# Heads: projections step first in a round, and those of tiles 2 to 4 begin two tiles ahead, with their queries in a score buffer

## The chip, the cores and the metric

The kernel runs on one core of a Trainium2 chip. A core has five engines that take their instructions in order from queues of their own and meet at semaphores: TensorE (matmuls, transposes), VectorE, ScalarE, GpSimd, and SyncE, which here only issues DMA transfers. The metric is device time in microseconds for one launch, the median of the runs. All data are fp32.

## The reference

Two layers act on 3327 nodes of 256 features: a graph convolution, a mixture of experts, a graph attention, and last a block of attention heads, which is all that the change touches:

```python
# x: (3327, 256), layer-normed; 4 heads (n), 4 experts (e) of queries per head, d = 64
sx = einsum('bsh,ndh->bnsd', x, hl_w) + hl_b
q  = einsum('bnsd,neod->bneso', sx, wq)
k  = einsum('bnsd,nod->bnso', sx, wk)
v  = einsum('bnsd,nod->bnso', sx, wv)
scores = einsum('bnesd,bntd->bnest', q, k) * d**0.5 + causal
att = softmax(scores, axis=-1)
qkv = einsum('bnest,bntd->bnesd', att, v)          # zero where sx is zero
# then a gate over the 4 experts, residual, layer norm, a two-layer FFN with
# residual and layer norm, and a softmax gate over the heads
```

The mask is causal: a tile of rows sees only itself and the tiles before it. So the work grows along the sequence, and the first tiles have very little.

## The kernel before

The rows are padded to 3328 and cut into 26 tiles of 128. The earlier layers leave their result in a DRAM tensor `xs`; then `heads` (line 854) runs the block. It writes every instruction in the order in which it is to stand: the wrapper `InOrder` chains each engine's instructions, so that each engine's queue is the order of the program, and line 61 (inside the wrapper) is the line of all of them in the profile. Tiles have to be told apart by names.

**Projections.** `prepare(t, res)` (line 907) makes what tile t needs. It is a generator with nine steps between its `yield`s: 1, load the rows (`xres`, a SyncE transfer); 2, their mean and variance on VectorE (`pst`, `pmv`, `prs`); 3, the norm on GpSimd (`prs`, `xn`); 4, transpose on TensorE, and copy (`pt`, `xt`); 5, the heads' input (`psxt`, `sxt`), and its nonzero mask `nz` by two ScalarE operations; 6, four transfers that lay the mask out as `sxd`, and the values (`pv`, copied to `v`); 7, the keys (`pk`, copied to `kt`), and four transfers of `v` to the DRAM tensor `vs`; 8, the queries (`pq`, copied with a factor 8 to `qt`); 9, the transpose of `sxt` back to rows (`sx`), and `res.update(...)`, which makes "qt" a key of the tile's entry in `ready`. `empty` (line 877) gives each copy to ScalarE or VectorE by a running sum of their loads. Some buffers are single: `xn` and `nz` share one tag with one buffer, so `xn` of a next tile can be written only when the transfers that read the last `nz` are over. `xt` and `v` are single, `sxt` and `xres` double, `sxd` triple, `qt` double.

**Attention.** A unit is a head of a tile (lines 1374, 1375), in order of tiles. Its keys are cut in `t // 4 + 1` chunks of up to 512 columns. For a chunk, `fill` makes the scores of the four experts on TensorE (`pqk`, four PSUM banks), `drain` brings them to a score buffer `sc` on VectorE with their maximum (a masked form for the last chunk), `weigh` takes the exponential on ScalarE, `turn` transposes 32x32 blocks on VectorE in place, `values` loads the values from `vs` to `vr`, and `attend` multiplies on TensorE into `po`. After a unit's last chunk `over` masks `po` into `ot`, and `back` transposes it (`ptO`) and copies it (`qkv`, `glp`). The pool `scp` has nine score buffers, of 4x512 numbers a partition. One pool `psm` of four PSUM banks serves `pqk` and all other small matmuls.

**Tails.** When a tile's four heads are through, `tail` (line 1193), again a generator, makes gate, norms, FFN and output, mostly on GpSimd and ScalarE.

**Order.** The main loop (line 1422) is one round per chunk: drain ahead as far as `wanted` says (three chunks, and `t // 4` more), attend, turn the next chunk, load and weigh the second next, `back` of the unit that has ended, one step of the tails and one of the projections, the rest of the weighing, and one `fill` if none is left. For tiles below 8 tails and projections step in every round, later only in rounds that follow no unit's end. `begin(u)` (line 1376) is called by the first `fill` of a unit. For the first head of a tile it steps the tile's generator until it is over, and starts that of the next tile. A tile of the first four has four rounds, so half of the nine steps of `prepare` are left to this forced end; tiles 4 to 7 have eight rounds.

Of the kernel before, what the change touches and what calls it, by code (L numbers as in the profile page):

```python
# [12 lines left out]
F32 = mybir.dt.float32  # L13
# [9 lines left out]
P = 128  # L23
N = 3327
NT = 26
# [3 lines left out]
BLK = 512  # L29
# [72 lines left out]
class Net:  # L102
# [751 lines left out]
    def heads(self, xs, vs, out):  # L854
# [3 lines left out]
        with ExitStack() as ctx:  # L858
            one = ctx.enter_context(tc.tile_pool(name="at", bufs=1))
            self.work = ctx.enter_context(tc.tile_pool(name="atw", bufs=2))  # L860
            scp = ctx.enter_context(tc.tile_pool(name="ats", bufs=9))
            vrp = ctx.enter_context(tc.tile_pool(name="atv", bufs=3))
            tl = ctx.enter_context(tc.tile_pool(name="att", bufs=2))
# [43 lines left out]
            def prepare(t, res):  # L907
# [63 lines left out]
                        in_=v[ds(Q * b, Q), :, :],  # L971
                    )
                yield
                qt = tl.tile([P, 4, 2, P], F32, tag="qt", name="qt")
                pp = [ps.tile([P, 2, 2, P], F32, tag="b", name="pq") for _ in range(2)]
                for c in range(2):
                    for i in range(2):
# [13 lines left out]
            def run(gens):  # L991

                gens[:] = [g for g in gens if next(g, None) is None and g.gi_frame is not None]

            tails, preps, ready = [], [], {}

# [48 lines left out]
            def weigh(u, g, experts):  # L1047

                n = span(u["t"], g)[1] * P
                q = ready[u["t"]]  # L1050
                if u["h"] == g == 0 and 0 in experts:
                    q["den"] = sm.tile([P, 16, 7], F32, tag="den", name="aden", bufs=2)
                for k in experts:
                    e = u["sc"][g][:, k, :n]
                    nc.scalar.activation(
                        e, e, AF.Exp, bias=u["nmax"][:, k : k + 1],
                        accum_out=q["den"][:, 4 * u["h"] + k, g : g + 1],
                    )
                    load["act"] += 0.26 + 0.00088 * n

            def values(u, g):

                lo, n = (4 * i for i in span(u["t"], g))
                v = u["v", g] = vrp.tile([P, 16, 64], F32, tag="vr", name="vr")
                for q in range(4):
                    nc.sync.dma_start(out=v[ds(Q * q, Q), :n, :], in_=vs[u["h"], :, lo : lo + n, :])

            def turn(u, g):


                n = span(u["t"], g)[1] * P
                w = u["sc"][g][:, :, :n]
                nc.vector.transpose(w, w)
                load["dve"] += 0.1 + 0.00417 * n
# [7 lines left out]
            def attend(u, g):  # L1082


                t = u["t"]
                w, v = u["sc"][g], u["v", g]
                lo, n = (4 * i for i in span(t, g))
                for b2 in range(0, n, 2):
                    for k in range(2):
                        for q in range(4):  # L1090
                            r, b = ds(Q * q, Q), b2 + k

                            after = 4 * t + q - lo
                            if b > after and t:
                                continue
                            nc.tensor.matmul(
                                po[ds(64 * k, 64), q, :, :], v[r, b, :], w[r, :, ts(b, Q)],
                                start=(g == b2 == 0), stop=(b + 2 > after if t else b2 == 2),
                            )

            def over(u):

                u["ot"] = tl.tile([P, 4, P], F32, tag="ot", name="ot", bufs=1)
                to = u["ot"].rearrange("p e (q i) -> p q e i", q=4)
                there = u["sxd"][:, u["h"] : u["h"] + 1, :]
                if u["t"] < 5 or u is units[-1]:

                    nc.vector.tensor_tensor(
                        to, po,
                        there.rearrange("p o (q i) -> p q o i", q=4).to_broadcast([P, 4, 4, Q]),  # L1110
                        ALU.mult,
                    )
                    load["dve"] += 0.7
                else:
                    nc.scalar.copy(to, po)
                    nc.gpsimd.tensor_tensor(
                        u["ot"], u["ot"], there.to_broadcast([P, 4, P]), ALU.mult
                    )
                    load["act"] += 0.6

            def back(u):


                h = u["h"]
                r = ready[u["t"]]
                if h == 0:
                    r["qkv"] = tl.tile([P, 4, 4, 64], F32, tag="qkv", name="qkv", bufs=2)
                    r["glp"] = sm.tile([P, 4, 4, 4], F32, tag="glp", name="glp", bufs=3)
                pt = ps.tile([P, 4, 68], F32, tag="b", name="ptO")
                for e in range(4):  # L1130
                    nc.tensor.matmul(
                        pt[:, e, :], u["ot"][:, e, :], igw[:, h, e, :], start=True, stop=True
                    )
                nc.scalar.copy(r["qkv"][:, h, :, :], pt[:, :, :64])
                nc.scalar.copy(r["glp"][:, h, :, :], pt[:, :, 64:])
                load["act"] += 0.55
                if u["t"] == NT - 1:
                    if h % 2:
                        tails.append(last_tail(u["t"], h // 2, u["sx"], r))
                elif h == 3:  # L1140
                    while len(tails) > 4:
                        run(tails)
                    tails.append(tail(u["t"], u["sx"], r["qkv"], r["glp"], r["den"]))
# [232 lines left out]
            def begin(u):  # L1376

                t = u["t"]
                if u["h"] == 0:
                    while preps:  # L1380
                        run(preps)
                    if t == 0:
                        for _ in prepare(0, ready.setdefault(0, {})):
                            pass
                    if t + 1 < NT:
                        preps.append(prepare(t + 1, ready.setdefault(t + 1, {})))
                u.update(ready[t])

            filled = drained = 0
# [1 line left out]
            def fill_next():  # L1391
                nonlocal filled
                if filled < len(chunks):
                    u, g = chunks[filled]
                    if g == 0:
                        begin(u)
                    fill(u, g)
                    filled += 1

            def drain_to(n):  # L1400
                nonlocal drained
                while drained < min(n, len(chunks)):
                    if filled == drained:
                        fill_next()
                    drain(*chunks[drained])
                    drained += 1

            def wanted(k):

                return k + 3 + chunks[min(k + 2, len(chunks) - 1)][0]["t"] // 4  # L1410
# [11 lines left out]
            for k, (u, g) in enumerate(chunks):  # L1422
                ahead = chunks[k + 2] if k + 2 < len(chunks) else None
                drain_to(wanted(k))
                attend(u, g)
                if k + 1 < len(chunks):
                    turn(*chunks[k + 1])
                if ahead:
                    values(*ahead)
                    if ahead[1]:  # L1430
                        weigh(*ahead, range(2))
                if ended:
                    back(ended)
                last = u if g == u["t"] // 4 else None
                if last:
                    over(u)
                if not ended or u["t"] < 8:
                    run(tails)
                    run(preps)
                ended = last  # L1440
                if ahead:
                    weigh(*ahead, range(2 if ahead[1] else 0, 4))
                if filled == drained:
                    fill_next()
# [556 lines left out]
```

## Time and profile before

| what | value |
| --- | --- |
| median of 3 runs | 2971.8 us (2970.73 to 2976.79) |
| the profiled execution's own time | 2971.83 us |
| its span | 2970.1 us |
| TensorE busy | 2662.9 us, 90% |
| VectorE busy | 2398.0 us, 81% |
| ScalarE busy | 1813.9 us, 61% |
| GpSimd busy | 973.8 us, 33% |
| mean granted TensorE clock | 0.973 |
| first instruction of the heads | 973.41 us, the transfer of `xres` |

In the profile PE is TensorE's matmuls, PEld its loads of weights, DVE is VectorE, ACT ScalarE, POOL GpSimd, and SPq the transfers that SyncE issues. A line of the view in order of time has the start and the length in us, engine, line, operation, what is written and what is read with shapes, and how many; in brackets stands how long the engine was idle before it, and what it was released by. A group merges instructions that follow each other. A matmul of fp32 data appears twice in the counts[...]. Ends of matmuls are modelled, so TensorE's busy time is not time at its peak rate.

The main loop follows no clock: which engine waits is decided by the order of queues, and by buffers.

### The profile page before, as it was taken

The numbers are of one execution on the slowest core, as the hardware profiler recorded it, in microseconds if no ns is written. First come the engines' busy times: TensorE is split into PE (matmuls) and PEld (weight loads), VectorE is DVE, ScalarE is ACT, GpSimd is POOL, SyncE is SP. The second block draws the span as 40 slices with busy tenths as digits, with TensorE's granted clock in tenths as the row PEclk, the third lists the DMA queues.
The fourth block names the chain that finished last, engine by engine and source line by source line (L and its number), as shares of the span: only waits on it lengthen the run. The fifth ranks groups of instructions, "written<-read, shape, count | busy, mean of one in ns | idle before, by whom it ended". The sixth has DMA issues, their size and how long they took to land. (4 is left out here: it accounts for less than half of the span.)

```text
span 2970.1 us, 125328 instructions
## 1 busy us (share of the span) xinstructions
PE 2662.9 (90%) x53422; PEld 1966.3 (66%) x53422; DVE 2398.0 (81%) x5619; ACT 1813.9 (61%) x5128; POOL 973.8 (33%) x1448
## 2 busy tenths in 40 slices
PE   7999988879889788899999999999989999999996
PEld 6878887657668666566666666666666666656664
DVE  5102643689999577789999999999999999999997
ACT  6410135555555457677777776777777677676674
POOL 6441635622231146544433332322222222122121
PEclk9999999999999789999999999999999999999997
DMA  9994568648775222333333443443433433343432
GB/s 377 355 321 135 185 220 276 226 159 285 243 251 169 56 77 77 104 100 106 114 107 104 116 115 106 115 114 112 122 112 113 117 114 114 111 118 110 117 109 77
DMA packets 258188, 449.70 MB, mean 151 GB/s; under 512 B 58816, under 2 KB 156608, under 8 KB 257504
## 3 DMA queue, kind: packets, MB, share of 16 engines
q1 hardware_dynamic: 245536, 417.50, 45.6%
q0 software_dynamic: 6576, 18.02, 1.7%
q8 instruction: 421, 6.90, 1.0%
q10 hardware_dynamic: 5520, 6.18, 0.7%
q14 instruction: 135, 1.11, 0.1%
HBM read 393.37 MB, written 25.88 MB: 141 GB/s over the span
## 5 line engine op out<-in xcount | busy, mean ns | idle before, releaser
L61 ACT ACTIVATE sc<-sc,anmax 128x512 f32<-128x512 f32 (+3 forms) x1568 | 1040.4, 668 | 109.6 <-DVE anmax L61 109.4
L61 PEld LDWEIGHTS po<-sc,vr 32*64 32x64 f32 x43728 | 662.8, 131 | 395.2 <-DVE sc L61 234.0
L61 PE MATMUL po<-sc,vr 32*64 32x128 f32 x43728 | 765.2, 275 | 117.7 <-DVE sc L61 72.3
L61 DVE STREAM_TRANSPOSE sc<-sc 128x2048 f32<-128x2048 f32 (+3 forms) x392 | 816.2, 2082 | 24.2 <-ACT sc L61 23.9
L61 PE MATMUL pqk<-kt,qt 64*128 64x512 f32 (+3 forms) x3136 | 776.2, 579 | 24.5 <-ACT qt L61 4.8
L61 DVE TENSOR_SCALAR_CACHE_REDUCE sc<-pqk 128x512 f32<-128x512 f32 (+2 forms) x1152 | 655.5, 623 | 76.7 <-PE pqk L61 74.7
L61 PEld LDWEIGHTS pqk<-kt,qt 64*128 64x128 f32 x3136 | 319.2, 187 | 247.0 <-issue 102.5
L61 PE MATMUL acc<-wh,p 128*128 128x259 f32 x1352 | 310.0, 387 | 34.5 <-DVE p L61 34.4
L61 PEld LDWEIGHTS acc<-wh,p 128*128 128x128 f32 x1352 | 254.1, 190 | 92.7 <-DVE p L61 52.2
L61 PE MATMUL acc<-y,pan 128*128 128x256 f32 x1352 | 303.5, 385 | 12.2 <-DMA pan<-in_adjt_dram 10.5
L61 POOL TENSOR_TENSOR ot<-ot,sxd 128x512 f32<-128x512 f32 x83 | 105.7, 1273 | 601.1 <-ACT ot L61 588.2
L61 ACT ACTIVATION_READ_ACCUMULATOR sc<-sc,anmax 128x1 f32 x1568 | 299.4, 191 | 0.0
L61 PEld LDWEIGHTS acc<-y,pan 128*128 128x128 f32 x1352 | 257.8, 192 | 53.0 <-issue 17.5
L61 DVE CUSTOM_DVE_ANT_0 sc<-pqk,mask 128x512 f32<-128x512 f32 (+3 forms) x416 | 242.1, 636 | 38.4 <-PE pqk L61 38.0
L61 ACT ACTIVATE u<-u,d 128x512 f32<-128x512 f32 (+1 forms) x182 | 125.2, 688 | 159.4 <-DVE u L61 159.3
L61 DVE SCALAR_TENSOR_TENSOR u<-bc,d 128x512 f32<-128x512 f32 (+1 forms) x182 | 136.4, 750 | 0.1
L61 DVE SCALAR_TENSOR_TENSOR p<-pan,u 128x512 f32<-128x512 f32 (+1 forms) x182 | 126.9, 697 | 10.2 <-PE acc L61 6.1
L61 ACT COPY qkv<-ptO 128x256 f32<-128x256 f32 x104 | 38.5, 370 | 153.3 <-PE ptO L61 153.0
L61 ACT ACTIVATE junk<-ar 128x1664 bf16<-128x1664 f32 x52 | 82.7, 1591 | 65.9 <-DMA ar<-in_adj_dram 64.8
L61 PE MATMUL ptO<-igw,ot 128*128 128x68 f32 x832 | 117.2, 284 | 5.5 <-issue 2.3
L61 PEld LDWEIGHTS ptO<-igw,ot 128*128 128x128 f32 x832 | 102.4, 193 | 24.1 <-issue 17.5
L61 DVE CUSTOM_DVE_ANT_0 sg<-sg,dst 128x1664 bf16<-128x1664 bf16 (+2 forms) x56 | 99.9, 1791 | 1.2 <-ACT dst L61 1.0
(336 smaller groups left out, 2976.6 us busy)
## 6 DMA issues: line engine op xcount, KB each, us to landing
vr<-vs SPq DMA_DIRECT2D x976, 128.0 KB
ar<-in_adj_dram SPq DMA_DIRECT2D x104, 832.0 KB
vr<-vs SPq DMA_DIRECT2D x544, 96.0 KB
pan<-in_adjt_dram SPq DMA_DIRECT2D x156, 256.0 KB
pan<-in_adjt_dram SPq DMA_DIRECT2D x26, 1024.0 KB
pan<-in_adjt_dram SPq DMA_DIRECT2D x20, 832.0 KB
w1e<-w SPq DMA_DIRECT2D x59, 256.0 KB
took<-places SPq DMA_DIRECT2D x59, 129.0 KB
```

What stands on the lines that cost most here:

```text
L61: made = make(*args, **kw)
```

## The change

`run(preps)` now stands ahead of `run(tails)` in a round. Tiles 2, 3 and 4 have their generators started two tiles ahead (that of tile 2 together with that of tile 1, four rounds later); from tile 5 on it is one tile ahead as before. `begin` steps all running generators only until the tile that begins has its queries, no longer until all are over. The queries of tiles 0 to 4 are put into a buffer of the score pool, half of which they use, so that three tiles' queries can be alive at once.

```diff
@@ prepare
-                qt = tl.tile([P, 4, 2, P], F32, tag="qt", name="qt")
+                if t < AHEAD:
+                    qt = scp.tile([P, 4, BLK], F32, tag="sc", name="qts")[:, :, : 2 * P]
+                    qt = qt.rearrange("p h (i q) -> p h i q", i=2)
+                else:
+                    qt = tl.tile([P, 4, 2, P], F32, tag="qt", name="qt")
@@ heads
             tails, preps, ready = [], [], {}
+            AHEAD = 5
+            def later(n, gen):
+                for _ in range(n):
+                    yield
+                yield from gen
@@ begin
                 if u["h"] == 0:
-                    while preps:
-                        run(preps)
                     if t == 0:
                         for _ in prepare(0, ready.setdefault(0, {})):
                             pass
-                    if t + 1 < NT:
-                        preps.append(prepare(t + 1, ready.setdefault(t + 1, {})))
+                    while preps and "qt" not in ready[t]:
+                        run(preps)
+                    begun = [t + 1] if AHEAD <= t + 1 < NT else []
+                    if t + 2 < AHEAD:
+                        begun = [t + 2] if t else [1, 2]
+                    for i, n in enumerate(begun):
+                        preps.append(later(4 * i, prepare(n, ready.setdefault(n, {}))))
@@ the main loop
                 if not ended or u["t"] < 8:
+                    run(preps)
                     run(tails)
-                    run(preps)
```

The profile of the changed kernel calls the queries of tiles 0 to 4 `qts`.

## The prediction

> **What bounds the kernel now.** I read the page's slices first, then stretches cut at the tiles of the last stage, then TensorE and VectorE in order of time across one tile boundary, and last the waits on `xn`. The chain of waits on the page reaches back only over the last tenth of the span, so it says nothing on the place of the change.
>
> The slices (74.3 us each; tenths of VectorE busy, then TensorE's granted clock):
>
> ```profile
> DVE  5102643689999577789999999999999999999997
> PEclk9999999999999789999999999999999999999997
> ```
>
> From slice 18 (1337 us) to the last but one VectorE is at nine tenths or more; there is hardly anything to win there. The stage of the heads begins at 973 us, and its first five slices stand at 5, 7, 7, 7, 8, with the clock at 7 and 8 in two of them. Cut from one tile's first score matmul to the next one's (columns: stretch, length, then busy time and count of PE, PEld, DVE, ACT, POOL, then clock, DMA share, GB/s):
>
> ```profile
> 1010.45:1032.99 22.54, 19.71 (x272) 15.73 (x272) 14.80 (x55) 13.49 (x52) 1.74 (x3) 0.83 0.26 69
> 1032.99:1061.30 28.31, 22.88 (x376) 17.56 (x376) 19.44 (x57) 17.10 (x61) 10.91 (x16) 0.84 0.28 77
> 1061.30:1095.30 34.00, 27.59 (x511) 20.04 (x511) 23.71 (x57) 20.91 (x67) 11.66 (x17) 0.85 0.28 79
> ```
>
> These are tiles 1, 2, 3. VectorE idles 7.74, 8.87 and 10.29 us, TensorE 2.83, 5.43 and 6.41. The idle time is nearly one piece per tile, the forced end of `prepare`; here from tile 2 to tile 3:
>
> ```profile
> 1053.24 0.65 DVE L61 TENSOR_TENSOR ot<-po,sxd 128x512 f32<-128x512 f32 x1
> 1053.88 2.07 PE L61 MATMUL psxt<-xt,hlt 128*128 128x128 f32 x8 [2.49 <-ACT xt L61]
> 1056.54 1.22 PE L61 MATMUL pv<-wv,sxt 128*128 128x128 f32 x4 [0.58 <-ACT sxt L61]
> 1057.69 1.23 PE L61 MATMUL pk<-sxt,wk 64*128 64x128 f32 x8
> 1058.70 1.92 PE L61 MATMUL pq<-sxt,wq 64*128 64x128 f32 x16
> 1060.65 1.08 ACT L61 ACTIVATE qt<-pq 128x512 f32<-128x512 f32 x2 [1.06 <-PE pq L61]
> 1061.30 2.57 PE L61 MATMUL pqk<-kt,qt 64*128 64x512 f32 x8
> 1063.05 0.69 DVE L61 CUSTOM_DVE_ANT_0 sc<-pqk,mask 128x512 f32<-128x512 f32 x1 [9.15 <-PE pqk L61]
> ```
>
> VectorE stops for 9.15 us while TensorE walks a serial chain. The same gap opens tiles 1, 2 and 4, with 8.09 (plus 1.28 and 1.06), 7.03 and 9.28 us.
>
> Later a second, smaller wait: TensorE stands at the transpose of `xn`, which GpSimd makes late (tiles 6 to 9: 1.92, 4.80, 3.85, 1.41 us). The seventh and eighth:
>
> ```profile
> 1206.20 0.69 PE L61 MATMUL pt<-ident,xn 128*128 128x128 f32 x2 [4.80 <-POOL xn L61]
> 1208.50 0.56 DVE L61 TENSOR_SCALAR_CACHE_REDUCE sc<-pqk 128x384 f32<-128x384 f32 x1 [3.01 <-PE pqk L61]
> 1257.51 0.69 PE L61 MATMUL pt<-ident,xn 128*128 128x128 f32 x2 [3.85 <-POOL xn L61]
> 1260.24 0.69 DVE L61 TENSOR_SCALAR_CACHE_REDUCE sc<-pqk 128x512 f32<-128x512 f32 x1 [3.44 <-PE pqk L61]
> ```
>
> [...] `psxt` takes 2.07 us in the gaps and 1.06 in the running stream (1265.55), the pair of transposes 0.69 against 0.44. [...] the first `xres`, issued at 973.41, released VectorE at 975.45, 2.04 us.
>
> **The change, part by part.** No instruction is added but a few queue entries; order and one buffer differ.
>
> (1) *Tile 1, a loss.* The forced rounds at `begin(1)` now also step tile 2's generator. In TensorE's queue the transpose of `xn` of tile 2 and its `psxt` come to stand ahead of tile 1's first scores. That `xn` has the single buffer which `nz` of tile 1 holds until its four `sxd` transfers have landed. They were issued 1006.86 to 1009.41; plus 2.0 is 11.4, plus two GpSimd operations of 0.60 and 0.61 gives 1012.65. TensorE, done with `pq` at 1009.77, waits 2.9 us; then transposes 0.69, `xt` copy 0.37 and hand-over 0.1, `psxt` 2.07: scores at 1015.85 instead of 1010.45. **+5.4.** Queued behind it are tile 1's scores, so VectorE as well. If the nz buffer came free early this is +3; with a late landing +8.
>
> (2) *Tile 1 to 2.* Before, first drain to first drain was 1011.60 to 1033.94 = 22.34, of it 7.03 gap and 15.3 VectorE work in an unbroken row. Now the rest of tile 2's projections and the first steps of tile 3's lie in these rounds: TensorE +0.7 (`pv`), +0.7 (`pk`), +1.2 (`pq`), +0.9 (two pairs of transposes), at running-clock durations. A round is `pqk` 1.3, `po` 1.2, `ptO` 1.1 = 3.6 on TensorE against 3.4 to 5 on VectorE; the additions lengthen it by about 1.2 in all. 16.5 against 22.3: **−5.8**, which just pays for (1).
>
> (3) *Tile 2 to 3.* 29.11 before, 9.15 gap, 20.0 work without a break. TensorE's 22.88 busy contains the chain at half clock, 6.5 to 7.1 us by its rows (2.07+1.22+1.23+1.92+0.69), which become 4.1 in the stream (1.06+0.69+0.72+1.16+0.44). Rounds stretch by 0.6 (round 1: 3.7+1.06 against 4.1). One forced round stays at `begin(3)`: `sx` of tile 3 and `psxt` of tile 4, the latter waiting for an `xt` copied behind two `qts` copies (1.08+0.37). VectorE's cover is transpose and `ot`, 2.4; 2 us remain open. 22.6: **−6.5**.
>
> (4) *Tile 3 to 4.* 33.50 before, 9.28 gap; 24.2 work, rounds of 6 us against TensorE's 4.7 to 5.1 plus 0.4 to 1.2: hidden. +0.5 for stretching: **−8.8**. At tile 5 the forced `pq` remains; ScalarE's `kt` copies (0.63) leave the wait behind `nzf`: **−0.5**, of a gap of 7.10.
>
> (5) *Projections first, tiles 6 to 9.* In the built order `prs` and `xn` stand ahead of seven operations of the second norm (GpSimd 1199.88 to 1204.32, 4.4 us; for tile 6 ten, 6.7). The waits 1.92, 4.80, 3.85, 1.41 fall to 0, 0.4, 0, 0: 11.6 us of TensorE. VectorE's gaps right after are 0.55, 3.01, 3.44, 1.03 = **−8.0** (bounds −5 and −11.6). What is late next is the norm, by 1.8 us; two empty rounds stand before its transpose, so nobody waits.
>
> (6) *Score buffers, SyncE.* At most three of nine buffers hold queries; four chunks of scores are alive in tiles 0 to 3, five in tile 4. Nobody waits: 0. Without that room VectorE would wait a round, 4 us. On SyncE the `vr` loads pass behind four `sxd` (2.6) or four `vs` issues (2.0), but are wanted two rounds later, 7 us: 0; without that cover 2 us per tile, three times.
>
> (7) *From tile 5 on* the order within a round changes on ScalarE and GpSimd alone: 0, with −5 and +6 as ends (rivals).
>
> Sum: 5.4 −5.8 −6.5 −8.8 −0.5 −8.0 = **−24.2**. The profiled execution took 2971.83 (span 2970.1), the same as the median 2971.8; so 2947.6, say **2948**.
>
> **Rivals.**
>
> *TensorE becomes the bound of tiles 1 to 3.* For: it is busy 19.71 of 22.54. If its busy time does not shrink, its idle 2.83+5.43+6.41 = 14.7 is all there is, less 5.4, and half of (5): −13, **2959**. Against: some 7 us of each tile were chain at half clock. A weaker form, in which the 5.4 grows to 10, leaves −8.
>
> *It doesn't do what it says.* Forced rounds remain, and the gap only moves to where `xt`, `kt` or a bank is awaited, as tile 5's 7.10 shows with all its rounds. Then (3), (4) and (5) shrink to a third, 7.8, against +5.4 −5.8: −8 or less, **2966** to 2972.
>
> *Slower: ScalarE waits in order.* A projection's copy now stands ahead of a tail's work that is ready, so ScalarE waits for the matmuls of that step: 4.5 us a tile (1.06+0.7+0.7+1.16+0.44+0.44), 21 tiles, 94.5 at most. From 26% of it reaching VectorE (24.2) the gain is gone; a third, 31.5, gives **2979**. For: ScalarE's `qkv` copies wait for TensorE's `ptO` already, 77.5 us past 1400 us. Against: it is busy 61%, and past 1330 us VectorE waited for ScalarE's `sc` for only 14.7 us, so there is slack.
>
> *More than forecast:* (1) at +3 and (5) at its full 11.6, with tile 3's round hidden: −32, **2940**.
>
> **How the numbers follow.** The forecast (2938 to 2960, the first rival's number inside) 0.67; above 35 us of gain 0.06; the weak gain, 2960 to 2966, 0.14; within 0.2% (6 us, about what a measurement of this kernel can tell from no change) 0.07; slower 0.06. Faster: 0.67+0.06+0.14 = 0.87. The range for 8 in 10 is 2935 to 2963: it leaves out half of the weak gains, the unchanged, the slower, and a tail of the large gains.
>
> **What would show it.** VectorE's gaps at the first drains of tiles 2, 3 and 4 below 3 us; that of tile 1 grown from 8 towards 16, with TensorE waiting there for GpSimd's `xn`; `psxt` at about 1.06 us from tile 3 on; waits of `pt` on `xn` in tiles 6 to 9 near zero; tile 4's first drain some 16 us earlier, tile 10's some 24, and the shift constant after. Wrong if tile 1's gap passes 25 us, if new VectorE gaps on ScalarE's `sc` appear past 1330 us, or if a drain waits for a score buffer.

## The result

The changed kernel takes 2943.3 us (median of five runs, 2939.7 to 2954.3) against 2971.8 of the kernel before (2963.2 to 2976.8). The ratio is 0.9916, with an interval from 0.9889 to 0.9943. In a second set of runs it was 2946.6 against 2974.5, ratio 0.9907 [0.9890, 0.9923]. Faster, then: the medians differ by 28 us, where 24 were forecast.

To see where they come from I use one mark for each tile: the start of VectorE's first masked drain of that tile, counted from the start of the first `xres` transfer, with which the stage of the heads begins. The stages ahead of it hold the same code in all kernels here, yet in fourteen profiled executions the heads began anywhere from 972.9 to 981.6 us. Marks counted from the stage's own start leave that out. The change against before, in us:

| mark | before | change | difference | change, second execution |
|---|---|---|---|---|
| tile 1 | 38.19 | 42.78 | +4.6 | +4.4 |
| tile 2 | 60.53 | 59.08 | −1.5 | −1.9 |
| tile 3 | 89.64 | 83.31 | −6.3 | −6.7 |
| tile 4 | 124.58 | 109.81 | −14.8 | −15.2 |
| tile 5 | 170.86 | 156.65 | −14.2 | −14.0 |
| tile 10 | 433.52 | 408.69 | −24.8 | −25.4 |
| tile 13 | 632.67 | 608.37 | −24.3 | −24.1 |
| tile 16 | 877.55 | 844.60 | −33.0 | −30.8 |
| end | 1996.72 | 1964.06 | −32.7 | −32.8 |

The profiled execution of the change spans 2941.6 us, 28.5 less than before: 32.7 won in the heads, 4.2 lost in the stages ahead, which the change doesn't touch.

The slices of the page of the kernel after, VectorE's busy tenths and TensorE's granted clock:

```profile
DVE  5102643589999587889989999999999999999997
PEclk9999999999999799999999999999999999999998
```

The first slices of the heads (the fourteenth on) stood at 5, 7, 7, 7, 8 and stand at 5, 8, 7, 8, 8; the clock is held down in one slice instead of two. Cut into stretches close to the first score matmuls of the tiles (columns as before: stretch, length, busy time and count of PE, PEld, DVE, ACT, POOL, then clock, DMA share, GB/s), tiles 1, 2, 3 of the kernel after:

```profile
1019.10:1035.50 16.40, 16.15 (x267) 12.69 (x265) 14.06 (x53) 10.93 (x40) 1.74 (x3) 0.98 0.35 93
1035.50:1060.00 24.50, 21.62 (x389) 16.66 (x389) 20.60 (x59) 16.91 (x62) 6.82 (x9) 1.00 0.39 108
1060.00:1087.00 27.00, 25.14 (x511) 17.95 (x511) 24.40 (x60) 20.50 (x67) 9.94 (x14) 1.00 0.33 90
```

They took 22.54, 28.31 and 34.00 us. (The cuts are rounded, and the last one lies 2.8 us behind tile 4's first scores, at 1084.24, so the third stretch is a little too long here.) VectorE's busy time is about what it was (14.80, 19.44, 23.71); its idle time fell from 7.74, 8.87, 10.29 to 2.34, 3.90, 2.60. The granted clock rose from 0.83 to 0.85 there to 0.98 and 1.00. In the chains of projections at the old gaps of tiles 2, 3 and 4 (1026.05 to 1032.20, 1053.90 to 1060.70 and 1087.45 to 1094.50 in the kernel before) it had been 0.53, 0.50 and 0.50.

The same in order of time, the lines that answer to those shown of before. First the start of tile 1, which is now later, then the first drains of tiles 2 and 3 and the gap that stays at tile 5:

```profile
1015.02 0.61 POOL L61 TENSOR_TENSOR xn<-xres,pmv 128x256 f32<-128x256 f32 x1 [8.66 <-DMA sxd<-nz]
1016.38 0.69 PE L61 MATMUL pt<-ident,xn 128*128 128x128 f32 x2 [3.00 <-POOL xn L61]
1017.52 2.08 PE L61 MATMUL psxt<-xt,hlt 128*128 128x128 f32 x8
1019.53 1.48 PE L61 MATMUL pqk<-kt,qts 64*128 64x256 f32 x8
1020.36 0.42 DVE L61 CUSTOM_DVE_ANT_0 sc<-pqk,mask 128x256 f32<-128x256 f32 x1 [2.41 <-PE pqk L61]
...
1036.65 0.56 DVE L61 CUSTOM_DVE_ANT_0 sc<-pqk,mask 128x384 f32<-128x384 f32 x1 [0.29 <-PE pqk L61]
...
1058.63 1.16 PE L61 MATMUL psxt<-xt,hlt 128*128 128x128 f32 x8 [0.85 <-ACT xt L61]
1060.88 0.69 DVE L61 CUSTOM_DVE_ANT_0 sc<-pqk,mask 128x512 f32<-128x512 f32 x1 [2.05 <-PE pqk L61]
...
1128.74 0.56 DVE L61 TENSOR_SCALAR_CACHE_REDUCE sc<-pqk 128x384 f32<-128x384 f32 x1 [6.79 <-PE pqk L61]
```

`xn` of tile 2 waits for the four `sxd` transfers out of `nz`, TensorE waits 3.00 us for `xn`, and tile 1's scores stand behind it. The gaps of 7.03 and 9.15 us at tiles 2 and 3 are 0.29 and 2.05; at tile 4 there is none; tile 5's 7.10 is 6.79.

### The profile page after: what moved, and what is told of

Same layout as the page of the kernel before. It is cut to its first block, busy times and chain, and to the rows that moved or that the text cites. A ratio compares the mean times of both kernels' runs of the same rounds, so it can differ in the third digit from the quotient of the medians.

```text
span 2941.6 us, 125324 instructions
## 1 busy us (share of the span) xinstructions
PE 2652.3 (90%) x53422; PEld 1963.2 (67%) x53422; DVE 2398.5 (82%) x5619; ACT 1811.3 (62%) x5128; POOL 973.1 (33%) x1448
## 3 DMA queue, kind: packets, MB, share of 16 engines
q14 instruction: 135, 1.11, 0.1%
## 5 line engine op out<-in xcount | busy, mean ns | idle before, releaser
L61 PE MATMUL pqk<-kt,qt 64*128 64x512 f32 (+1 forms) x2944 | 738.4, 582 | 18.6 <-ACT qt L61 5.3
L61 PEld LDWEIGHTS pqk<-kt,qt 64*128 64x128 f32 x2944 | 299.3, 185 | 230.3 <-issue 99.2
L61 DVE CUSTOM_DVE_ANT_0 sc<-pqk,mask 128x512 f32<-128x512 f32 (+3 forms) x416 | 242.3, 636 | 24.2 <-PE pqk L61 23.7
```

The source lines that it names most:

```text
L61: made = make(*args, **kw)
```

## Experiments

Each ran beside the kernel before; the medians are of 4 to 16 executions. The edits are told below. The three kernels with masks of tails apart (the one with tiles 6 and 7 ahead is one of them) also have `nz` of tile 1 apart and tile 5 ahead.

| kernel | median us | ratio to before, interval |
|---|---|---|
| the change | 2943.34 | 0.9916 [0.9889, 0.9943] |
| exchange only | 2958.20 | 0.9944 [0.9929, 0.9959] |
| early start only | 2965.31 | 0.9974 [0.9966, 0.9983] |
| `nz` of tiles 0 to 4 apart | 2946.32 | 0.9908 [0.9892, 0.9925] |
| tile 5 ahead too | 2947.11 | 0.9909 [0.9895, 0.9923] |
| projections first from tile 10 on | 2960.71 | 0.9950 [0.9937, 0.9962] |
| `nz` of tile 1 apart | 2943.96 | 0.9893 [0.9878, 0.9907] |
| eight score buffers | 3058.01 | 1.0286 [1.0265, 1.0307] |
| masks of tails 3 to 5 apart | 2948.53 | 0.9907 [0.9889, 0.9924] |
| masks of tails 2 to 5 apart | 2935.89 | 0.9869 [0.9850, 0.9888] |
| tiles 6 and 7 ahead too | 2936.91 | 0.9880 [0.9862, 0.9898] |
| the change again | 2946.60 | 0.9907 [0.9890, 0.9923] |
| masks of tails 2 to 5 apart, again | 2941.28 | 0.9889 [0.9873, 0.9906] |

### The two halves of the change

Exchange only (the kernel before with this edit):

```diff
-                    run(tails)
                     run(preps)
+                    run(tails)
```

> The kernel before, with only the two calls in the main loop exchanged, so that projections step ahead of tails. Marks are the first drains of tiles, counted from the first transfer of the heads; before: tile 1 38.2, tile 4 124.6, tile 6 215.1, tile 10 433.5, tile 13 632.7, tile 16 877.6, tile 25 1842.6. My theory (two parts that add, the exchange is worth 8 us in tiles 5 to 9): marks of tiles 1 to 4 within 1 us of before, tile 10 earlier by 8.5 (425), and the time 2963. If the further 8 us that the changed kernel gains between tiles 13 and 16 also come from the exchange, tile 16 is earlier by 16 (861) and the time 2955; if they are chance or come from the early start, tile 16 is earlier by 8.5. Rival (ScalarE waits in order for a projection's matmuls): marks fall back after tile 10, tile 25 no earlier than before. Rival (TensorE is the bound): tile 10 earlier by 4 or less.

Early start only (the changed kernel with that edit undone):

> The changed kernel with tails ahead of projections again, so the early start alone. My theory: tile 1 later by 4.6, tile 2 earlier by 1.4, tile 3 by 6.3, tile 4 by about 14.5, tile 10 still by about 15, and the time 2957. Rival (the early start needs the exchange, since a projection behind a tail waits on GpSimd and ScalarE): tile 4 earlier by less than 9, time over 2962. If the gain between tiles 13 and 16 comes from the early start: tile 16 earlier by 23, time 2949.

The exchange alone won 15.0 us in the stage: 2.4 by tile 4, 10.1 more from tile 5 to tile 10 (262.7 us became 252.5), and 5.6 from tile 13 to tile 16, of which 2.7 were gone again at the end. The 2.4 us by tile 4 are more than the 1 us that was expected; their cause isn't shown. The early start alone moved tile 1 by +4.8 and tile 4 by −13.2, but its end only by −8.7: from tile 5 to tile 10 it won 1.2 us, and from tile 16 to tile 25 that execution took 969.5 us against 965.0, at the upper end of the 963.5 to 969.3 that this stretch took in twelve other executions (all but that with eight score buffers, below). Its time, 2965.3 us, is 8 above the 2957 that was expected; but tile 4 gained more than 9 us, so the early start doesn't need the exchange, as the rival had it. The two ratios, −0.56% and −0.26%, add to −0.82%, the change's −0.84%, and the marks add too up to tile 10 (−12.7 and −12.6; the change −24.8 and −25.4). At the end of these single executions they don't: −15.0 and −8.7 against −32.7. So as far as the intervals tell, the parts don't depend on each other much. The exchange, a swap of two lines, is the larger one.

### Where the gain past tile 13 comes from

Nothing in the prediction has a gain there. The waits of TensorE's weight loads and of VectorE, tile 13 to tile 16 (columns: engine and operation, what it waited for, us in total, times, longest), of the kernel before:

```profile
PEld pqk L61 <- ACT kt L61: 6.7, 3, 2.6
...
DVE sc L61 <- PE pqk L61: 14.0, 15, 2.9
```

and of the kernel after:

```profile
PEld pqk L61 <- ACT kt L61: 1.8, 3, 0.9
...
DVE sc L61 <- PE pqk L61: 6.7, 9, 1.7
```

In order of time, one of these waits in the kernel before:

```profile
1640.18 0.35 ACT L61 ACTIVATE sq<-fo,l2ns 128x64 f32<-128x64 f32 x1
1640.43 0.19 ACT L61 ACTIVATION_READ_ACCUMULATOR sq<-fo,l2ns 128x1 f32 x1
1640.53 0.62 ACT L61 COPY kt<-pk 128x256 f32<-128x256 f32 x2
...
1640.93 1.13 PE L61 MATMUL pqk<-kt,qt 64*128 64x512 f32 x4 [1.25 <-ACT kt L61]
```

ScalarE copies the keys `kt` only after the squares of a tail's second norm, and the scores of the round wait for `kt`. With projections first the copy stands ahead of the tail. That another engine makes the copies isn't the reason: ScalarE makes 49 of the 52 key copies both in the kernel before and with the exchange alone. The same division runs through all fourteen executions: with tails first there (the kernel before, and the early start alone) the weight loads of `pqk` wait 6.7 us for `kt` in this stretch, with projections first 1.8 to 2.1. To see that this belongs to the exchange, and not to the early start or to chance, tails were left first up to tile 9:

```diff
+                    first, second = (tails, preps) if u["t"] < 10 else (preps, tails)
-                    run(preps)
-                    run(tails)
+                    run(first)
+                    run(second)
```

> The change, but with the tails' steps first again in tiles 0 to 9; projections come first only from tile 10 on. If the gain past tile 12 belongs to the exchange (ScalarE's copies of the keys no longer stand behind a tail's work): tile 10's first masked drain as with the early start alone (about 421 us after the stage's first transfer), the stretch from tile 13 to tile 16 at 239 instead of 244.8 us, TensorE's and its weight loads' waits for the keys' copy there from 10.9 us to none, about 2960 us. If that stretch was shorter by chance or through the early start: 244.8 again, 2965 us.

Tile 10 came at 420.6, as with the early start alone, and tile 13 to 16 took 241.0 us; the wait for `kt` fell to 1.8 us, not to none. In the twelve executions with projections first there, this stretch took 236.2 to 242.2, on average 239.6; in the two with tails first, 244.9 and 244.7. The exchange is worth some 5 us in this stretch. This run's own profiled execution shows less of it at the next mark: from tile 10 to tile 13 it took 201.7 us, where the thirteen others took 198.8 to 200.5, so at tile 16 it stood only 1.2 us ahead of the early start alone, and 1.5 at the end. That execution was the slowest of the six; their median, 2960.7 us, is that which was expected. Of the change's 8.6, the 3 beyond the average seem to be that execution's own: its repetition showed 6.7.

> The change itself once more, beside the next run on the same chip. In its first profiled execution the stretch from tile 13 to tile 16 took 236.2 us; the seven other kernels with projections first there took 239 to 242, the two with tails first 244.8. If the late gain of the exchange is 5 us and the rest was chance, the stretch takes 239 to 242 us here and the time is 0.991 to 0.993 of before; if the change has something there that the variants lack, 236 again.

The second execution took 238.2 us there, a little below the variants' range that was given.

### Tile 1's loss, and what became of its cure

`nz` of tiles 0 to 4 was put in the idle half of the score buffer that holds the queries, so that `xn` of the next tile need not wait for the `sxd` transfers:

```diff
-                nz = self.work.tile([P, 2, P], F32, tag="xn", name="nz", bufs=1)
+                if t < AHEAD:
+                    room = scp.tile([P, 4, BLK], F32, tag="sc", name="qts")
+                    nz = room[:, 0:2, 2 * P : 3 * P]
+                else:
+                    nz = self.work.tile([P, 2, P], F32, tag="xn", name="nz", bufs=1)
...
-                    qt = scp.tile([P, 4, BLK], F32, tag="sc", name="qts")[:, :, : 2 * P]
+                    qt = room[:, :, : 2 * P]
```

> The changed kernel; for tiles 0 to 4 the mask nz is written to the half of the query's score buffer that lay idle, so that the norm xn no longer shares a buffer with it. My theory (the first step, the loss at tile 1 is the wait of xn for the landing of four sxd transfers): GpSimd's wait of 8.66 us on these transfers and TensorE's 3.00 us at the transpose of xn before tile 1 are gone; tile 1 at 39.9 instead of 42.8 (what is left over 38.2 is psxt of tile 2 ahead of the scores), tiles 2 to 10 earlier by 2 to 3 than in the changed kernel, time 2941. Rival (the loss is the psxt and the order of TensorE's queue alone): tile 1 at 42 or more. Rival (VectorE's rounds after it absorb the start): tile 1 earlier, tile 4 the same as in the changed kernel.

Tile 1 came at 39.7 instead of 42.8, and tiles 2 and 3 were 2.9 and 3.1 us earlier too: the wait for the transfers is the cause of 3 of tile 1's 4.6. But from tile 3 to tile 4 this kernel needed 32.4 us where the change needs 26.5, so that tile 4 came 2.8 us later than in the change. TensorE in order of time there:

```profile
1053.07 1.13 PE L61 MATMUL pqk<-kt,qts 64*128 64x512 f32 x4
1056.49 2.59 PE L61 MATMUL pqk<-kt,qts 64*128 64x512 f32 x4 [2.29 <-ACT sx L61]
1059.01 2.86 PE L61 MATMUL po<-sc,vr 32*64 32x128 f32 x84
1061.80 1.98 PE L61 MATMUL ptO<-igw,ot 128*128 128x68 f32 x8
1063.57 1.16 PE L61 MATMUL pv<-wv,sxt 128*128 128x128 f32 x4
1064.65 3.04 PE L61 MATMUL pqk<-kt,qts 64*128 64x512 f32 x8
```

The second half of tile 3's first scores waits 2.29 us for ScalarE's copy of `sx`; in the change the same four matmuls waited 0.79 us, for VectorE. The order of TensorE's instructions is the same in both; but this matmul waits for ScalarE in one and for VectorE in the other. That points to another PSUM buffer; the traces don't show the buffers themselves. After the pause TensorE's matmuls took longer: these rows take 2.59, 2.86, 1.98, 1.16 and 3.04 us, in the change, at a granted clock of 1.00 there, 1.73, 1.64, 1.11, 0.66 and 1.99, a difference of 4.5 us; with the 1.5 us of longer pause that is the whole loss of 5.9, to 0.1.

If so, the cure works where the scores of tile 3 keep their PSUM buffer. With `nz` apart for tile 1 alone (`if t == 1` in the edit above) they wait for VectorE again.

> The change, with the mask nz of tile 1 alone in the idle half of the queries' score buffer (with all of tiles 0 to 4 the gain of tile 1 was lost again between tiles 3 and 4, where TensorE waited 2.3 us for ScalarE's copy of sx [...]). My theory: that loss came from another PSUM buffer that the scores of tile 3 got there, not from being earlier. Then tile 1's first masked drain lies at 39.7 instead of 42.8, tile 2's at 56, tile 3's at 80, tile 4's at 106.7 (26.5 after tile 3's), and the time is 3 us below the change, 2940. Rival: whatever is early there is lost by tile 4: 112 there, 2946 us.

Tiles 1 to 4 came at 39.4, 56.3, 80.3 and 106.8 us, with 26.5 from tile 3 to tile 4. The loss was the wait and the slow matmuls after it, not the earliness. The 3 us stay to tile 10 (−4.1 against the change); at the end of that execution 1.6 are left, and in time the two kernels can't be told apart.

### Do the queries take room from the scores?

```diff
-            scp = ctx.enter_context(tc.tile_pool(name="ats", bufs=9))
+            scp = ctx.enter_context(tc.tile_pool(name="ats", bufs=8))
```

> The change with eight score buffers in place of nine. If the three buffers that hold queries cost the scores nothing (step 6), the first masked drains of tiles 1 to 10 stay within 2 us of the change's, and a loss, if any, comes in tiles 24 and 25 alone, where nine chunks are alive: 2943 to 2951 us. If the scores were already short of room with queries in three of nine, taking one more away costs a round of some 4 us in tiles 2 to 5: tile 6 at 206 instead of 201.7, 2948 to 2956 us.

Tile 10 came at 408.3 (change: 408.7), tile 23 at 1565.1 (1563.4): in the tiles where queries lie in score buffers, even one buffer fewer costs nothing. Then tile 24 alone, mark to mark, took 185.9 us instead of 126.5, tile 25, from its first masked drain to its last, 143.8 instead of 99.1. I had placed this loss rightly, where nine chunks are alive, and given it 8 us at most; in the stage it is 112. VectorE's waits from 2650 us on:

```profile
DVE sc L61 <- PE po L61: 106.7, 49, 4.7
```

and one of them in order of time:

```profile
2849.44 1.81 PE L61 MATMUL pqk<-kt,qt 64*128 64x512 f32 x5
2852.35 2.10 PE L61 MATMUL po<-sc,vr 32*64 32x128 f32 x128 [1.10 <-DVE sc L61]
2854.48 0.69 DVE L61 CUSTOM_DVE_ANT_0 sc<-pqk,mask 128x512 f32<-128x512 f32 x1 [2.19 <-PE po L61]
```

Each drain waits for the weighted sum `po` that frees the oldest buffer, and that one waited for VectorE's transpose: the two engines take turns, and VectorE waits 2.2 us on average at 49 drains. In the change VectorE has no such wait in these tiles.

### The gap that stays at tile 5

First, tile 5 was begun two tiles ahead as well:

```diff
-            AHEAD = 5
+            AHEAD = 6
```

> The changed kernel with AHEAD = 6: tile 5 too is begun two tiles ahead, its queries in a score buffer. My theory (the gap of 6.8 us at tile 5's first drain is the forced last steps, with ScalarE's kt and query copies behind a tail's nzf): the gap falls under 2 us, tile 5 and all later ones earlier by 5 to 6 than in the changed kernel, time 2938. Rival (TensorE or ScalarE is full in tile 4, so the work moved there lengthens its rounds): tile 5 earlier by less than 2. Rival (too few score buffers in tile 4): a drain or query copy waits for an attend, tile 5 later.

Tile 4 to tile 5 took 44.5 us instead of 46.8, but tile 5 to tile 6 took 48.0 instead of 45.1. The forced walk is gone, and this stands in its place:

```profile
1124.02 0.72 POOL L61 TENSOR_TENSOR fo<-fo,nzf 128x256 f32<-128x256 f32 x1
1124.78 0.42 ACT L61 ACTIVATE nzf<-fx 128x256 f32<-128x256 f32 x1 [5.13 <-POOL fo L61]
1127.64 1.25 DVE L61 STREAM_TRANSPOSE sc<-sc 128x1024 f32<-128x1024 f32 x1 [5.48 <-ACT sc L61]
1129.11 2.78 PE L61 MATMUL pqk<-kt,qts 64*128 64x384 f32 x4 [4.07 <-ACT fot L61]
```

ScalarE, in order, stands 5.13 us before the mask `nzf` of one tail until GpSimd has multiplied with that of the tail before; there is one such buffer. Behind it wait the exponentials, and so VectorE, and the copy `fot`, and so TensorE. I gave the mask a score buffer in the tails of some early tiles (with `nz` of tile 1 apart and `AHEAD = 6`):

```diff
-                nz = tl.tile([P, 2, D], F32, tag="nzf", name="nzf", bufs=1)
+                if 3 <= t < 6:
+                    nz = scp.tile([P, 4, BLK], F32, tag="sc", name="nzs")[:, 0:2, :D]
+                else:
+                    nz = tl.tile([P, 2, D], F32, tag="nzf", name="nzf", bufs=1)
```

> As the run with tile 1's nz apart, with tile 5 also begun two tiles ahead, and the tails' mask nzf of tiles 3 to 5 in a score buffer of its own instead of the single nzf buffer. With tile 5 ahead alone, the forced gap of 6.8 us was replaced by one of 5.5, where ScalarE waited 5.1 us for GpSimd's last product with the previous tail's nzf. If that single buffer is the cause, the gap is gone: tile 6 some 5 us earlier than in the run with tile 1's nz apart, 2935 us. If GpSimd's chain to fot (TensorE waited 4.1 us for it) holds the scores anyway: no gain over that run, 2940 us.

No gain, and the wait of 5.11 us was still there, on a row named `nzf`, not `nzs`: the tail that waits at tile 5's start is tile 2's, which I had left on the single buffer. The run says nothing on the cause. With `2 <= t < 6`:

> As the run before with the tails' mask in a score buffer, but from tile 2's tail on: the wait of 5.1 us lay at tile 2's nzf, which still used the single buffer, so that run had not touched its cause. If the single nzf buffer is the cause (tile 2's mask waits for GpSimd's product of tile 1's tail with it), ScalarE goes on 5 us earlier, the gap of 5.5 us before tile 5's scores shrinks below 1.5 us, tile 6's first masked drain comes some 4 us before that of the run with tile 1's nz apart (193 instead of 196.8), and the time is 4 us below it. If GpSimd's chain holds the scores through fot, the gap only moves there: 3 us or more remain, tile 6 at 198 to 201.

```profile
1116.92 0.44 ACT L61 ACTIVATE nzs<-fx 128x256 f32<-128x256 f32 x1
1119.81 1.25 DVE L61 STREAM_TRANSPOSE sc<-sc 128x1024 f32<-128x1024 f32 x1 [0.26 <-ACT sc L61]
1120.69 0.44 PE L61 MATMUL pt<-ident,fo 128*128 128x128 f32 x2 [1.11 <-POOL fo L61]
```

ScalarE doesn't wait, VectorE's gap is 0.26 us instead of 5.48, and tile 6 comes at 190.7, 6.1 us before the run with `nz` of tile 1 apart and 11.0 before the change. The single mask buffer was the cause: the two runs differ in nothing but tile 2's mask. With tiles 6 and 7 ahead too (`AHEAD = 8`, masks `2 <= t < 8`):

> The same with tiles 6 and 7 also begun two tiles ahead (their queries in score buffers too) and the tails' masks of tiles 2 to 7 apart. The forced round at the start of tiles 6 and 7 goes. If such a round costs TensorE's chain of sx and the copy of the queries, 1 to 2 us each, tile 8's first masked drain comes 2 to 4 us earlier than in the run just before. If one forced round is hidden behind VectorE's work, or the scores lack the room that the queries take in tiles 5 to 7 (five chunks alive, four buffers held), there is no gain, or a loss of some 4 us a tile.

Tile 5 came 3.6 us later, tile 8 3.5 later, and the end 0.9 earlier: no gain. From tile 4 to tile 6 VectorE waited 10.4 us for ScalarE's exponentials (at most 2.83 us at once), where it had been 6.7; whether for room or for the added steps wasn't separated.

The version with the masks of tails 2 to 5 apart has the lowest median of all. It ran once more beside the change on one chip:

> The version with tile 1's nz apart, tile 5 begun ahead and the masks of the tails of tiles 2 to 5 apart, beside the change on the same chip. In the first execution it led the change by 11 us at tile 6, 10 at tile 13, but 4 at the end. If the 11 us are kept, it is 8 to 11 us below the change, 0.987 to 0.989 of before; if later stretches give them back, 4 us or less, 0.990.

2941.3 us against 2946.6, with intervals that overlap. The marks repeat: 9.8 us ahead of the change at tile 6, 9.4 at tile 13, 3.9 at the end (first time 11.0, 10.4, 3.6). Of 10 us won early, about 6 are given back from tile 13 on, in both executions. What gives them back stays open.

## Why the prediction was right, and where not

**Time and direction.** 2948 forecast, 2943.3 measured, inside the forecast's own range of 2938 to 2960. At tile 10, where the forecast has all of its gain, the change stands at −24.8 and −25.4 for −24.2; what came later was not forecast (7). The closeness at tile 10 is in part luck, though. The forecast gave 16.2 to the early start, parts (1) to (4), and 8.0 to the exchange; run alone they stand at −12.6 and −12.7 there. Two misses of some 4 us each cancel.

**(1) Tile 1, +5.4:** +4.6 measured. The chain is as it was told, down to TensorE's wait of 3.00 us (2.9). Taking `nz` apart removed 3 of it.

**(2) Tile 1 to 2, −5.8:** −6.0. The gap of 7.03 is 0.29.

**(3) Tile 2 to 3, −6.5:** −4.9. The 2 us that were to stay open at the forced round are there (2.05). The stretch took 24.2 and not 22.6. From drain to drain VectorE was busy for 19.75 (I had 20.0) and idle for 4.48: that gap and 2.4 in short pieces, the longest 0.96 for ScalarE's exponentials, where I had allowed 0.6 for stretched rounds. This is the term that was too small.

**(4) Tile 3 to 4, −8.8, and tile 5, −0.5:** −8.4 and +0.6. Tile 5's gap fell by 0.3 only.

**(5) The exchange in tiles 6 to 9, −8.0:** −10.6 in the change, −10.1 with the exchange alone, inside the bounds of −5 and −11.6. The waits of the transpose on `xn` became 0, 0.46, 0 and 0 at the named places.

**(6) Score buffers, 0:** held, even with one buffer fewer.

**(7) "From tile 5 on the order within a round changes on ScalarE and GpSimd alone: 0."** This step failed: it put at nothing what the new order does to ScalarE's copies. From tile 13 to tile 16 it was −8.6 and −6.7 in the two executions of the change, and −5 on average over the runs with projections first: before the change the copies of the keys stood behind tails on ScalarE all the way to tile 16, and after it the weight loads' wait for them fell from 6.7 to 1.8 us there. I had seen this at tile 5 (the `kt` copies behind `nzf`, 0.5 us) and had not followed it down. The slower rival feared the same in-order queue with the sign reversed: a projection's copy holding a tail. The waits of VectorE for ScalarE's exponentials, which would have shown that, stayed at 0.9 us from tile 13 to tile 16.

**Rivals.** TensorE was not the bound of tiles 1 to 3 at −13: its busy time did shrink, from 19.71, 22.88, 27.59 to 16.15, 21.62, 25.14, with the granted clock at 0.98, 1.00, 1.00 instead of 0.83, 0.84, 0.85. That the gap only moves was true of tile 5 alone, as its run with the earlier begin showed. "More than forecast" had the size of the stage's gain, −32, but by other terms.

**Durations at running clock.** The prediction priced the projections that moved into the rounds at the durations of the running stream, 1.06 us for `psxt` where the old gaps had 2.07. In the kernel before, the granted clock was 0.50 during the 2.07 us from 1053.88 and 1.00 during the 1.06 us from 1265.55. In the change `psxt` of tile 3 took 1.11 us and that of tile 4 1.16, both at 1.00; that of tile 2, after a pause of 3.00 us and the transposes, took 2.08 at 0.50. Step (1) also rests on the scores of tile 1 being held by the `psxt` ahead of them in TensorE's queue. They were: they began only at 1019.53, though their keys and queries had been copied by 1014.14.

## What to carry to other kernels

Where generators take turns in one round, their order decides what stands ahead in each engine's queue: step first what the scores of the same round wait for, and follow each of its copies through all stages, not only where a gap is seen. Before a step is begun earlier, look up what single buffer its inputs and its neighbours use; here `xn` with `nz`, and then `nzf`, took the place of the gap that was closed, and once, it seems, a PSUM buffer did. A spare buffer that is idle in early tiles can be the last one that late tiles need.

## What the runs showed of the hardware

A pause of TensorE can cost more than itself. With `nz` of tiles 0 to 4 apart, the matmuls after a pause of 2.29 us took 4.5 us longer in all than the same ones in the change, where the pause was 0.79 us.

Where the slow matmuls begin can differ between two kernels with the same pause. At tile 4 TensorE waited 1.91 us for ScalarE's `v` both in the change and with `nz` of tile 1 apart. The three groups that follow, `pqk` of 64x384 x4, `po` x64 and `ptO` x8, took 1.18, 1.97 and 1.88 us in the change, and 1.91, 1.94 and 1.11 in the other, where the last two take 1.21 and 1.11 shortly before the pause. So one pair of groups is slow in each, by about 1.5 us in all, but not the same pair. In the change the granted clock was 1.00 during the first of the three groups, 0.53 and 0.55 during the other two. What sets the place isn't shown.
